# The last eight sums of a graph attention kernel folded into two PSUM banks, and its last softmax stage issued earlier

## The chip, the cores and the metric

One core of a Trainium2 chip runs the program. Times are device microseconds (us); a median is that of three runs. One further execution of each kernel is recorded by the hardware profiler, and the rows of a profile come from that one.

## The reference

What is computed is one pre-norm graph attention layer over 12500 nodes of 128 numbers and 200000 edges, sorted by target, with 64 numbers each. There are 4 heads of 32.

```python
h    = maximum(layernorm(x), 0)                       # 12500 x 128
att  = a1.(W_node h)[src] + a2.(W_node h)[tgt] + a3.(W_edge edge)   # per edge and head
att  = where(att > 0, att, 0.2 * att)
m    = maximum(segment_max(att, tgt), 0)
ex   = exp(att - m[tgt])
den  = segment_sum(ex, tgt) + (200000 - deg) * exp(-m)
out  = x + segment_sum(ex / den[tgt] * (W_node h)[src], tgt)
```

The targets are sorted, so the edges of a node lie side by side, and where a group of edges ends inside a node, the next one continues it. Few edges fall on nodes at the end of the list: there a group of 511 edges touches up to 80 nodes.

## The kernel before, in words

The edges form 392 **groups** of 511 (four chunks of 128 columns each, the first column kept free), and four groups form one of 98 **quads**. Quads are softmaxed together in **supers**: two, two, then four at a time, and at the end 3, 3, 2, 2, 2, 2. The last super, s = 27, is quads 96 and 97; the one before is 94 and 95. All engines' orders are written by hand (`tc.manual_schedule()`): Python generators with `yield` between their steps are interleaved by `together` and `next`, and an engine executes in the order in which its instructions were issued.

The work on an edge has four parts.

*Rows.* A first phase writes the transformed rows of all nodes to a table in DRAM. POOL fetches the rows of an edge chunk by an indirect DMA (L177) into `ga`, which has room for eight quads; some chunks are fetched row by row from the queues of ACT and SP (L785).

*Logits.* For a quad, `all_logits` compares the targets with the nodes of the group's window (DVE L598), multiplies by the targets' shares (PE L604) and by the edge weights (PE L607), adds the pieces (`add_pieces`, DVE L616) and then the shares of the gathered rows (`add_sources`, DVE L628), which gives `U`. `flush` calls `add_sources` for the quad whose logits came last.

*Softmax of a super*, the turned stage (`softmax(s)`, with edges along the free axis): transposes of `U` into `t_ps` (PE L672), times 0.2 (ACT L674), the maximum of the two (DVE L677), a copy of it to `low` (ACT L681), a scan forward and one back with the mask `kp` (DVE L684, L685), which give each node's maximum inside its group; the ends of the groups are turned to one row (PE L695), scanned across the groups (DVE L702, L705) into `into` (L711) and turned back to a column (PE, then DVE copy L725); two more scans (DVE L727, L730) bring in what came from other groups; then the difference (DVE L734), the exponential `ex` (ACT L735), and transposes back (PE L744, L750). `kp` is made by `keeps(s)` from two neighbouring columns of the target list, one of them copied to PSUM first (ACT L653, DVE L655). `run_on(n)` issues n products whose results nobody reads (PE L644): 12 of them behind the ends of the last super, 2 later.

*Sums of a quad* (`sums(q)`): each group's rows are weighed by `ex` (DVE L908), 0/1 marks `hot` say which edge belongs to which node of the window (DVE L936; POOL L882 for the last two quads), and the products of marks and rows are added in a PSUM bank `acc` (PE L948). Row 0 of a bank is what the window's last node has so far; `carry` copies it (ACT L833) into the free first column of the next window's rows and adds the product of that chunk last (PE L840). `summed` copies the finished bank to `pt` (ACT L858) and takes the exponential of -m (ACT L864). `divide` then works out the shares (DVE L1001, L1004, L1006), multiplies (DVE L1010) and adds x (L1014), and the results are written, one window of rows at a time, by `issue` on SP's queue (L545). Windows of the last classes overlap: each is a group's 80 rows from its first node, whatever the number of its nodes, and a later write overwrites what an earlier one left beyond its nodes. The first 22 quads have one window of 80 rows each, those up to quad 35 one of 112 rows, those up to quad 74 one of 112 rows for two groups, and the rest, the last quads among them, a window of 80 rows for each group.

For the end of the program the order is special. In the last super, steps of `softmax` and of `sums(95)` alternate by hand; while `state["held"]` is set, the completion of quad 95's second group waits until the exponential of L735 is issued. The rows of x for quads 95, 96 and 97 are loaded in `sums(95)`. `weigh_last` weighs two groups of quad 97 on POOL (L908 with `last_ex`). A quad's last two groups are divided by themselves, or one by one in quad 97.

## Time and profile before

| | before |
|---|---|
| time, median of 3 runs (lowest to highest) | 1981.34 us (1979.71 to 1984.94) |
| the profiled execution: its time, its span | 1981.96 us, 1980.2 us |
| busy: POOL, PE, DVE, ACT | 1471.8 us (74%), 1338.1 us (68%), 1252.5 us (63%), 337.4 us (17%) |
| mean granted TensorE clock | 0.547 of full speed |
| HBM traffic over the span | 144 GB/s |
| gathers on POOL (L177) | 1463 of 945 ns, 1382.7 us |

The span runs from the first to the last instruction of the profiled execution; its time is 1.8 us more. POOL is the busiest engine and nearly all of its time is the issue of gathers. Over the steady part of the program no engine is above eight tenths in the 40 slices of the page, so what holds is read from the order of waits. The clock of PE is full in parts of the first phase and near the end, and half for most of what lies between.

### The profile page before, as it was taken

How to read it: one execution, taken by the hardware profiler on the slowest of the kernel's cores; microseconds unless marked ns; L12 is line 12 of the kernel's file. 1: busy time of each engine (PE TensorE's matmuls, PEld its weight loads, DVE VectorE, ACT ScalarE, POOL GpSimd, SP SyncE). 2: the span in 40 equal slices, each digit the busy share in tenths (PEclk: the TensorE clock that was granted, in tenths of full speed). 3: DMA queues.
4: the chain of work that ended last, by engine and by line, in shares of the span. 5: the costliest groups of instructions: out<-in, count | busy, mean ns of one | idle time of the engine just before them, and what ended most of it. 6: DMA issues, size and time to landing. Idle time of an engine off the chain costs nothing.

```text
span 1980.2 us, 33747 instructions
## 1 busy us (share of the span) xinstructions
PE 1338.1 (68%) x7385; PEld 1231.8 (62%) x7385; DVE 1252.5 (63%) x3393; ACT 337.4 (17%) x1121; POOL 1471.8 (74%) x1579
## 2 busy tenths in 40 slices
PE   6577786777657666667677576666665666777666
PEld 5466686766646556556566565666565665666655
DVE  6666766765655656557657566566566565667876
ACT  6655010110010100011101101111111011212222
POOL 7767767777777777777777777777777777777774
PEclk8757555555555555555555555555555555555557
DMA  7745655555545545455555555554645555555531
GB/s 257 205 112 123 163 143 136 136 140 165 152 131 165 148 145 151 133 170 152 145 162 147 157 146 158 148 167 135 171 124 134 143 133 137 127 152 128 151 96 34
DMA packets 158958, 288.26 MB, mean 146 GB/s; under 512 B 62488, under 2 KB 106103, under 8 KB 148368
## 3 DMA queue, kind: packets, MB, share of 16 engines
q1 hardware_dynamic: 103326, 174.78, 29.3%
q0 software_dynamic: 49120, 107.44, 23.4%
q10 hardware_dynamic: 6306, 3.85, 0.8%
q8 instruction: 61, 1.00, 0.2%
q14 instruction: 145, 1.19, 0.2%
HBM read 268.71 MB, written 17.19 MB: 144 GB/s over the span
## 4 chain that ended last, share of the span: by engine, by line
PE 29%; DVE 19%; POOL 15%; DMA 13%; issue 13%; ACT 4%; ACTq 4%; DVEq 0%; POOLq 0%
PE acc L948 15%; POOL ga L177 15%; DMA ga<-table,srci 13%; PE lg L607 7%; ACTq L785 3%; DVE at L598 3%; PE acc L840 2%; DVE ga L908 2%; DVE hot L936 2%; DVE t_ps L685 2%; DVE t_ps L684 2%; PE lg L604 1%; DVE t_ps L727 1%; DVE t_ps L730 1%; PE t_ps L672 1%
## 5 line engine op out<-in xcount | busy, mean ns | idle before, releaser
L177 POOL DMA_INDIRECT ga<-table,srci x1463 | 1382.7, 945 | 458.6 <-issue 358.2
L948 PE MATMUL acc<-ga,hot 128*113 128x137 f32 (+1 forms) x2724 | 713.2, 436 | 238.6 <-ACT ga L903 143.8
L948 PEld LDWEIGHTS acc<-ga,hot 128*113 128x113 f32 (+1 forms) x2724 | 589.3, 276 | 263.1 <-ACT ga L903 164.7
L607 PE MATMUL lg<-wblk,ea 128*128 128x8 f32 x1568 | 399.5, 352 | 0.0
L607 PEld LDWEIGHTS lg<-wblk,ea 128*128 128x128 f32 x1568 | 372.0, 301 | 0.0
L604 PEld LDWEIGHTS <-at 112*128 112x128 bf16 (+1 forms) x1568 | 218.4, 164 | 224.7 <-DVE at L598 202.7
L604 PE MATMUL lg<-pw,at 112*128 112x12 bf16 (+1 forms) x1568 | 170.3, 181 | 171.7 <-DVE at L598 171.4
L908 DVE TENSOR_TENSOR ga<-ga,ex_ps 128x528 f32<-128x528 f32 x390 | 269.1, 690 | 21.7 <-PE ex_ps L744 20.7
L598 DVE TENSOR_TENSOR at<-const_ps,db 112x512 bf16<-112x512 f32 (+1 forms) x392 | 264.8, 676 | 0.0
L936 DVE TENSOR_TENSOR hot<-const_ps,slot 128x448 f32<-128x448 f32 (+1 forms) x384 | 212.0, 552 | 0.0
L628 DVE TENSOR_TENSOR U<-const_ps,ga 128x64 f32<-128x64 f32 x98 | 26.1, 266 | 236.2 <-DMA ga<-table,srci 185.7
L840 PE MATMUL acc<-ga,hot 128*81 128x137 f32 (+1 forms) x412 | 133.7, 425 | 18.0 <-ACT ga L833 17.2
L975 DVE SCALAR_TENSOR_TENSOR den_of<-acc,den_of 113x4 f32<-113x4 f32 (+1 forms) x114 | 18.1, 159 | 193.4 <-ACT den_of L855 192.0
L840 PEld LDWEIGHTS acc<-ga,hot 128*81 128x81 f32 (+1 forms) x412 | 98.7, 271 | 26.2 <-ACT ga L833 24.8
L855 ACT ACTIVATE den_of<-acc 113x4 f32<-113x4 f32 (+1 forms) x114 | 19.6, 172 | 537.7 <-PE acc L948 315.6
L744 PE MATMUL ex_ps<-ident,ex 64*128 64x64 f32 (+2 forms) x112 | 18.6, 315 | 114.2 <-ACT ex L735 114.2
L744 PEld LDWEIGHTS ex_ps<-ident,ex 64*128 64x128 f32 (+2 forms) x112 | 13.8, 208 | 116.7 <-ACT ex L735 116.6
L177 POOL DMA_INDIRECT ga<-in_x_dram,srci x72 | 68.5, 952 | 23.2 <-issue 17.1
L833 ACT COPY ga<-acc 1x133 f32<-1x133 f32 x178 | 45.4, 255 | 202.1 <-issue 75.4
L858 ACT COPY pt<-acc 81x137 f32<-81x137 f32 x92 | 24.8, 269 | 219.0 <-PE acc L840 184.2
L435 PE MATMUL row_ps<-wcat,hT 128*128 128x137 f32 x198 | 41.1, 360 | 17.9 <-DVE tgt L441 7.9
L616 DVE TENSOR_REDUCE const_ps<-lg 128x64 f32<-128x192 f32 x98 | 35.0, 358 | 26.4 <-PE lg L607 25.8
(161 smaller groups left out, 1184.1 us busy)
## 6 DMA issues: line engine op xcount, KB each, us to landing
db<-in_dst_dram SPq DMA_DIRECT2D x53, 1024.0 KB
ea<-in_edge_t_dram SPq DMA_DIRECT2D x98, 512.0 KB
by_row<-table ACTq DMA_DIRECT2D x2304, 0.5 KB
db<-in_dst_dram SPq DMA_DIRECT2D x45, 640.0 KB
by_row<-table SPq DMA_DIRECT2D x1664, 0.5 KB
ga<-table,srci POOLq DMA_INDIRECT x1463
table<-row SPq DMA_DIRECT2D x9, 616.5 KB
xt<-in_x_dram SPq DMA_DIRECT2D x9, 576.0 KB
```

What stands on the lines that cost most here:

```text
L177: nc.gpsimd.indirect_dma_start(out=ga[:, i, j, 0:width], out_offset=None, in_=rows, in_offset=bass.IndirectOffsetOnAxis(ap=srci[:, g0 + i, ...
L435: nc.tensor.matmul(row_ps[:, t, :ROW], hT[:, t, :], wcat, start=True, stop=True)
L598: nc.vector.tensor_tensor(at[:span, i, :], node_ps[:span, w0 + i // k:w0 + i // k + 1].to_broadcast([span, GE]), db[:span, i, :], op=OP.is ...
L604: nc.tensor.matmul(lg[:, i, j].rearrange("p k h -> p (k h)"), at[:span, i, j * P:(j + 1) * P], sw, start=i + j == 0, stop=False, skip_grou ...
L607: nc.tensor.matmul(lg[:, i, 2 * w:2 * w + 2, 0, :], ea[:, i, w, :], wblk, start=False, stop=True, skip_group_check=True)
L684: nc.vector.tensor_tensor_scan(raw, same, att, initial=0.0, op0=OP.mult, op1=OP.max)
L785: row = engine.dma_start(as_bytes(to[p:p + 1, :]), rows_at(table, at[p % a_quad], 4 * ROW, 1))
L833: nc.scalar.copy(into, before[0:1, 0:R_CNT + 1])
L840: nc.tensor.matmul(acc, hot[:, i, 0, 0:acc.shape[0]], ga[:, i, 0, :], start=False, stop=stop)
L908: engine.tensor_tensor(val, val, weight.unsqueeze(3).to_broadcast([P, J, H, HW]), op=OP.mult)
L936: nc.vector.tensor_tensor(hot[:, i, :, 1:1 + span], lane_ps[:, 0:span].unsqueeze(1).to_broadcast([P, J, span]), slot[:, g, :].unsqueeze(2) ...
L948: nc.tensor.matmul(acc, hot[:, i, j, 0:1 + span], ga[:, i, j, :], start=new and j == 1, stop=i % k > 1 and i % k == k - 1 and j == J - 1)
```

## The change

Quads 96 and 97 leave `sums` and get a function of their own, `folded`. As before, each of their eight groups has its marks, its weighed rows and its own bank of sums over 81 rows. The bank is now copied to `pt` and multiplied by three 0/1 matrices, `SHIFT`, of 81 x 113: matrix b moves a group's row to the row that its node has in block b of the quad's window, which is 3 blocks of 112 nodes from the quad's first node. The products of a quad's four groups are added in one bank (113 rows, 3 x 137 columns), so that a node that two groups share is complete without a carry between them, and row 0 of the bank is the carry to the next quad. A quad has one exponential, one division and one write of 336 rows (three blocks of 112) in place of those per group. The matrices are made on DVE by comparing a row of lane numbers with the relative place of each node (`relative`, in the earlier check steps), during the sums of quads 92 and 93, in two slots of `ga` that no gather needs any more. x and the output are padded to 12928 rows for these windows.

Beside this: POOL makes the marks for groups 1 to 3 of quad 95 as well, and weighs three groups of quad 97 instead of two, from a copy of the exponentials in SBUF (`XE`). The steps of the last super's turned stage are issued ahead of the steps of `sums(95)` that stood between them: `add_sources` follows `add_pieces` at once, and the rest of `sums(95)`, groups 2 and 3, comes behind the stage. The hold of quad 95's second group is gone. Two steps that stood early are moved or dropped: the copy to `low` of the last super comes behind the two scans, and `keeps` reads the target list without the copy to PSUM for the first and last super. The loads of x for quads 96 and 97 are one each.

```diff
 CLASSES = (22, 4, NARROW), (36, 4, WIDE), (75, 2, WIDE), (None, 1, NARROW)
+FOLDS, PARTS, FREE = 2, 3, 3
...
+        nodes_at = lambda d, at: rows_at(d, at, 4 * D, PARTS * WIDE).rearrange(
+            "(b p) c -> p b c", p=WIDE)
...
+            if q >= first_fold:
+                at = ROWS[q] = windows(base_row, 4 * D, w, 1)
+                due["inputs"].append((as_bytes(xw[1:1 + WIDE, 0:PARTS, :]), nodes_at(x, at[0])))
+                return
...
-            before_ps = ps.tile([SBG * H, GE], F32, name="t_ps")
-            nc.scalar.copy(before_ps[:R], dr[:R, 0:NE + 1])
+            earlier = dr[:R, 0:NE + 1]
+            if 0 < s < len(supers) - 1:
+                before_ps = ps.tile([P, GE], F32, name="t_ps")
+                nc.scalar.copy(before_ps[:R], earlier)
+                earlier = before_ps[:R]
             kp = KP[s] = turned.tile([SBG * H, GE + 1], F32, name="kp")
-            nc.vector.tensor_tensor(kp[:R, 1:GE + 1], dr[:R, 1:NE + 2], before_ps[:R],
+            nc.vector.tensor_tensor(kp[:R, 1:GE + 1], dr[:R, 1:NE + 2], earlier,
                                     op=OP.is_equal)
...
-            raw = run_e if s == len(supers) - 1 else att
+            final = s == len(supers) - 1
+            if not final:
+                nc.scalar.copy(low[:R], att)
+            yield
+            raw = run_e if final else att
             nc.vector.tensor_tensor_scan(raw, same, att, initial=0.0, op0=OP.mult, op1=OP.max)
             nc.vector.tensor_tensor_scan(raw[:, ::-1], same_next[:, ::-1], raw[:, ::-1],
                                          initial=0.0, op0=OP.mult, op1=OP.max)
+            if final:
+                nc.scalar.copy(low[:R], att)
...
-            if state.pop("held", None):
-                complete_window(*begun.pop())
-                divide(*divisions.pop(0))
...
-            if s == len(supers) - 1:
+            if final:
                 run_on(2)
+                XE[s] = turned.tile([P, J, SBG * H], F32, name="xe")
+                nc.scalar.copy(XE[s][:, :, 0:R],
+                               ex_ps[:, 0:J * SBG * H].rearrange("p (j r) -> p j r", j=J)[:, :, 0:R])
...
-            if "held" in state and begun[-1][:2] == (nq - 3, 1):
-                divide(*divisions.pop(0))
-            division = divisions.pop(0) if divisions and "held" not in state else None
+            division = divisions.pop(0) if divisions else None
...
-            parts = {nq - 1: (2, 3), nq - 2: (2,), nq - 3: (2,), nq - 4: (2,)}.get(q, ())
+            parts = (2,) if first_fold - 2 <= q < first_fold else ()
...
-            if q >= nq - FREE:
-                for i in range(m):
+            if q >= first_fold - 1:
+                for i in range(0 if q >= first_fold else 1, m):
...
-            for a in range(nq - 3, nq) if q == nq - 3 else range(q + 1 if q else 0, min(q + 2, nq - 3)):
+            for a in range(q + 1 if q else 0, min(q + 2, first_fold)):
                 fetch_inputs(a)
-            if q == nq - 4:
+            if q == first_fold - 1:
+                for a in range(first_fold, nq):
+                    fetch_inputs(a)
+            if q == first_fold - 2:
                 issue("inputs", all_of=True)
...
-                if q == nq - 1 - FREE and i == 1:
-                    for a in range(nq - FREE, nq):
+                if q == first_fold - 1 and i == 1:
+                    for a in range(first_fold, nq):
                         HOT[a] = marks(a)
-                weigh(i + ahead)
-                if q < nq - FREE:
+                if first_fold - 4 <= q < first_fold - 4 + FOLDS:
+                    shifts(q + 4, i)
+                weighed(nc.vector, ga, i, heads(ex)[:, :, :, g - s0])
+                if q < first_fold - 1 or not i:
                     nc.vector.tensor_tensor(
                         hot[:, i, :, 1:1 + span],
                         lane_ps[:, 0:span].unsqueeze(1).to_broadcast([P, J, span]),
                         slot[:, g, :].unsqueeze(2).to_broadcast([P, J, span]), op=OP.is_equal)
-                if q == nq - 3 and i == 1:
-                    yield
...
-                if (q, i) == (nq - 2, 0):
-                    weigh_last()
-                issue("inputs", "results", *(["inputs"] * 3 if q == nq - 3 else []))
+                issue("inputs", "results", *(["inputs"] * 3 if q == first_fold - 1 else []))
...
+        SHIFT = {}
+        for a in range(first_fold, nq):
+            SHIFT[a] = ga_all[:, (a + 2) % QUADS].rearrange("p g j r -> p (g j r)")[
+                :, 0:QG * PARTS * (1 + WIDE)].rearrange("p (g b c) -> p g b c", b=PARTS, c=1 + WIDE)
...
+        def shifts(q, i):
+
+            to = SHIFT[q][:1 + NARROW, i]
+            R = 1 + NARROW
+            nc.vector.memset(to[:, :, 0:1], 0.0)
+            nc.vector.tensor_copy(to[:, 0, 0:1], ident[:R, 0:1])
+            nc.vector.tensor_tensor(
+                to[:, :, 1:1 + WIDE], lane_ps[:R].unsqueeze(1).to_broadcast([R, PARTS, WIDE]),
+                rel[:R, q - first_fold, i].unsqueeze(2).to_broadcast([R, PARTS, WIDE]),
+                op=OP.is_equal)
+
+        def folded(last_sums):
+            order = [(q, i) for q in range(first_fold, nq) for i in range(quads[q][1])]
...
+            together(last_sums)
+            complete()
+            for q, i in order:
+                on_gpsimd = q == nq - 1 and i < FREE
+                weighed(nc.gpsimd if on_gpsimd else nc.vector, rows[q], i,
+                        heads(XE[s] if on_gpsimd else ex)[:, :, :, quads[q][0] + i - s0])
+                if (q, i) == order[min(1, len(order) - 1)]:
+                    carried_in(first_fold, 0, rows[first_fold], fac if g_fold == s0 else None)
+            while divisions:
+                divide(*divisions.pop(0))
+            banks, accs, pts = {}, {}, {}
+
+            def chunks(q, i):
+
+                bank = ps.tile([P, 512], F32, name="acc", bufs=3)
+                accs[q, i] = bank[0:1 + NARROW, 0:ROW]
+                for j in range(0 if i else 1, J):
+                    nc.tensor.matmul(accs[q, i], HOT[q][:, i, j, 0:1 + NARROW], rows[q][:, i, j, :],
+                                     start=j == (0 if i else 1), stop=i > 0 and j == J - 1)
+
+            def copied(q, i):
+
+                if q not in pts:
+                    pts[q] = work.tile([P, QG, ROW], F32, name="pt", bufs=3)
+                nc.scalar.copy(pts[q][:1 + NARROW, i], accs.pop((q, i)))
+
+            def fold(q, i, last):
+
+                new = q not in banks
+                if new:
+                    banks[q] = (ps.tile([P, 512], F32, name="t_ps") if q == nq - 1 else
+                                ps.tile([P, 512], F32, name="ex_ps", bufs=2))
+                for b in range(PARTS):
+                    nc.tensor.matmul(banks[q][0:1 + WIDE, b * ROW:(b + 1) * ROW],
+                                     SHIFT[q][:1 + NARROW, i, b], pts[q][:1 + NARROW, i],
+                                     start=new and b == 0, stop=last, skip_group_check=True)
+
+            def shares(q):
+
+                acc = banks[q][0:1 + WIDE, 0:PARTS * ROW].rearrange("p (b r) -> p b r", r=ROW)
+                state["before"] = banks[q]
+                den = work.tile([P, QG, H], F32, name="den")[:1 + WIDE, 0:PARTS]
+                nc.scalar.activation(den, acc[:, :, R_SRC:R_SRC + H], AF.Exp, scale=-1.0)
+                return q, acc, den
+
+            def finish(q, acc, den):
+
+                R = 1 + WIDE
+                val = acc[:, :, 0:H * HW].rearrange("p b (h w) -> p b h w", w=HW)
+                nc.vector.scalar_tensor_tensor(
+                    den, acc[:, :, R_CNT:R_CNT + 1].to_broadcast([R, PARTS, H]), float(E), den,
+                    op0=OP.subtract, op1=OP.mult)
+                nc.vector.scalar_tensor_tensor(den, den, -1.0, val[:, :, :, HD],
+                                               op0=OP.mult, op1=OP.add)
+                nc.vector.reciprocal(den, den)
+                res = work.tile([P, QG, D], F32, name="res")[:R, 0:PARTS]
+                nc.vector.tensor_tensor(
+                    res.rearrange("p b (h d) -> p b h d", d=HD), val[:, :, :, 0:HD],
+                    den.unsqueeze(3).to_broadcast([R, PARTS, H, HD]), op=OP.mult)
+                nc.vector.tensor_tensor(res, res, XW[q][:R, 0:PARTS], op=OP.add)
+                due["results"].append((nodes_at(out, ROWS[q][0]), as_bytes(res[1:R])))
+                issue("results", all_of=True)
+
+            waits = []
+            for q in range(first_fold, nq):
+                g0, m = quads[q]
+                for i in range(m):
+                    chunks(q, i)
+                    if i == min(1, m - 1):
+                        if q > first_fold:
+                            carried_in(q, 0, rows[q], fac if g0 == s0 else None)
+                        nc.tensor.matmul(accs[q, 0], HOT[q][:, 0, 0, 0:1 + NARROW], rows[q][:, 0, 0, :],
+                                         start=False, stop=True)
+                        copied(q, 0)
+                    if i:
+                        copied(q, i)
+                    for a in waits:
+                        fold(*a)
+                    if waits and waits[-1][2]:
+                        ended = shares(waits[-1][0])
+                        finish(*ended)
+                    waits = [(q, 0, m == 1)] if i == 0 and m == 1 else [] if i == 0 else [
+                        (q, 0, False), (q, 1, m == 2)] if i == 1 else [(q, i, i == m - 1)]
+            for a in waits:
+                fold(*a)
+            finish(*shares(nq - 1))
...
-            add = nc.gpsimd if nq - 3 <= q <= nq - 2 and lo else nc.vector
-            add.tensor_tensor(res[:, :n, :], res[:, :n, :], xw, op=OP.add)
+            nc.vector.tensor_tensor(res[:, :n, :], res[:, :n, :], xw, op=OP.add)
...
 
                     next(turned_stage)
+                    next(turned_stage)
                     redo = nc.values_load(flag[0:1, 0:1], min_val=0, max_val=1)
                     next(beside[0])
-                    state["held"] = True
+                    next(turned_stage)
+                    next(turned_stage)
                     next(beside[0])
                     next(turned_stage)
                     next(beside[0])
+                    next(turned_stage)
+                    next(turned_stage)
+                    last_sums = beside[0]
+                    beside, turned_stage = [], iter(())
...
-            flush()
-            last_sums = sums(nq - 1)
-            together(last_sums)
-            complete()
-            complete()
+            folded(last_sums)
```

118 lines of the change are left out of this document (70 added, 48 removed).

## The prediction

> **What bounds the kernel now.** I read the page first (busy shares, costliest groups), then the timelines of POOL, SP, DVE, PE and ACT over the last 100 us, the chain that ended last, and the stretches of PE with their clock. In timelines and chain the columns are start, duration (both us), engine, line and tiles; brackets hold the idle time before and what ended it.
>
> ```profile
> span 1980.2 us, 33747 instructions
> ```
>
> ```profile
> 1933.70 0.94 POOL L177 DMA_INDIRECT ga<-table,srci  x1 [0.30 <-issue]
> 1934.69 16.10 POOL L882 TENSOR_SCALAR hot<-lane,slot 128x80 f32<-128x80 f32 x32
> ```
>
> POOL issues the gathers one after another, 0.94 us each with 0.30 us between, and the last ends at 1934.6. The change leaves their number and order alone, so up to there the time is given: what can move is the last 45.6 us. I read them backwards, from SP and DVE:
>
> ```profile
> 1966.82 10.46 SPq L545 DMA_DIRECT2D out_dram<-res  x6
> ```
>
> ```profile
> L545 SPq DMA_DIRECT2D out_dram<-res x16: 316/317/1526, 1936.9 to 1977.0; - x16
> ```
>
> ```profile
> SPq L545 <- DMA out_dram<-res: 22.8, 17, 2.9
> ```
>
> ```profile
> 1970.13 0.29 DVE L1014 TENSOR_TENSOR res<-res,inputs 81x128 f32<-81x128 f32 x1
> ```
>
> The last result is computed at 1970.4, yet the last write is issued at 1977.0. Writes of overlapping rows wait for one another (17 waits, 22.8 us), and the last six are issued (1977.0 - 1966.8) / 5 = 2.04 us apart. So DVE ends 9.8 us before the span does, and 3.2 us of that are the last write and the program's end. Ahead lie the turned stage (the softmax of quads 96 and 97) and their sums:
>
> ```profile
> 1937.46 0.37 DVE L616 TENSOR_REDUCE const_ps<-lg 128x64 f32<-128x192 f32 x1 [1.22 <-PE lg L607]
> ...
> 1940.14 0.26 DVE L628 TENSOR_TENSOR U<-const_ps,ga 128x64 f32<-128x64 f32 x1
> ...
> 1946.68 1.21 DVE L684 TENSOR_TENSOR_SCAN run<-kp,t_ps 32x511 f32<-32x511 f32 x1 [1.40 <-ACT low L681]
> ...
> 1949.77 0.22 DVE L702 TENSOR_TENSOR_SCAN ends<-thru,tops,ex_ps 1x8 f32<-1x8 f32 x1 [0.32 <-PE ex_ps L695]
> ...
> 1950.72 0.25 DVE L711 COPY into<-ends 1x32 f32<-1x32 f32 x2
> ```
>
> ```profile
> 1941.19 1.06 PE L672 MATMUL t_ps<-ident,U 128*32 128x128 f32 x4
> ...
> 1951.23 4.95 PE L644 MATMUL lg<-ones,ident 128*128 128x128 f32 x24
> ...
> 1958.15 1.61 PE L948 MATMUL acc<-ga,hot 128*81 128x137 f32 x12 [0.20 <-issue]
> ```
>
> ```profile
> 1942.29 0.58 ACT L674 ACTIVATE low<-t_ps 32x511 f32<-32x511 f32 x1
> ...
> 1954.85 0.63 ACT L735 ACTIVATE ex<-ex 32x511 f32<-32x511 f32 x1 [3.39 <-DVE ex L734]
> ```
>
> The stage runs from L616 at 1937.5 to the exponential of L735 at 1954.85; the first products of quad 96 start at 1958.15.
>
> **The change, part by part.**
>
> *Writes.* Eight writes of 80 rows become two of 336. Quad 95's four remain; at 2.04 us apart they are through before quad 96's is due, and that one before the last. Only the last stands behind DVE's end.
>
> ```profile
> 1942.48 3.97 SPq L545 DMA_DIRECT2D inputs<-in_x_dram  x8
> ```
>
> ```profile
> 1976.00:1977.00 1.00, 0.00 (x0) 0.00 (x0) 0.00 (x0) 0.00 (x0) 0.00 (x0) 0.50 0.16 41
> ```
>
> The second row is a stretch of one us (busy time of the engines, then clock, DMA share, GB/s): a write of 40 KB keeps the 16 DMA engines busy for 0.16 us. 4.2 times that is 0.67, so the larger write costs 0.5 us more. Bounds: nothing, or 2.0 us, half of what eight loads of 40 KB took in the first row. I take 0.5, since those loads were held by their issue. From DVE's end to the span's: 9.8 becomes 3.2 + 0.5 = 3.7. The loads of x for the two quads become two instead of eight, issued by SP about 20 us before they are read.
>
> *Fold products.* 24 products of 113x137, contracted over 81 partitions, come onto PE; the 32 products that make the sums of the eight groups stay.
>
> ```profile
> 1957.52 0.62 DVE ga L908
> ...
> 1963.88 0.28 ACT pt L858
> ...
> 1964.38 0.16 ACT ga L833
> ...
> 1964.59 0.46 PE acc L840 x2
> 1965.05 0.70 PE acc L948 x6
> ...
> 1966.36 0.22 ACT den L864
> ...
> 1966.61 0.17 DVE den L1001
> ...
> 1966.80 0.18 DVE den L1004
> ...
> 1967.00 0.22 DVE const_ps L1006
> ```
>
> ```profile
> 1967.75 0.42 DVE L1014 TENSOR_TENSOR res<-res,inputs 81x256 f32<-81x256 f32 x1
> ```
>
> Six records are three products: 0.233 us each at the full clock. The moving side of a fold is also 137 wide, so I give it the same price (bounds: half of that, or the 0.46 us of a product that comes alone). 56 x 0.233 = 13.05 us. PE is then full and ACT's copies (0.28 us) hide behind it, with one exception. In the built order the copy of row 0 from quad 96's bank into quad 97 stands behind DVE's multiplication by the shares: 0.22 + 0.17 + 0.18 + 0.22 + 0.55, the copy 0.2, with hand-overs 1.8 us, against 0.93 us of the four products that PE has meanwhile. PE waits 0.85 us. After the last fold come 0.15 us to land, the exponential 0.22, and on DVE 0.17 + 0.18 + 0.22 + two operations on 384 elements at 0.55 each (0.29 for 128, 0.42 for 256), with gaps 1.8. From the first product of quad 96 to DVE's end: 13.05 + 0.85 + 0.15 + 0.22 + 1.8 = 16.1 us, before 1970.4 - 1958.15 = 12.3. A loss of 3.8.
>
> *The turned stage first.* U now follows L616 directly: over at 1937.7 instead of 1940.4, if the gather of quad 97 has landed. Then transposes (0.9), ACT's scaling (0.6), the maximum (0.6), two scans (1.21 each) and the two columns (0.2) end at 1942.6, where L702's row has them ready at 1949.4: ACT's copy between maximum and scan is moved behind the scan, so the wait of 1.40 us goes too. But a weighing (0.62) and a division of quad 94 (0.17 + 0.18 + 0.22 + 0.42 + 0.42, with gaps 1.5) now stand before the 1.2 us from L702 to L711: `into` is ready at 1946.0 instead of 1951.0, 5 us earlier.
>
> Most of that is given back. On ACT the exponential of L735 now queues behind the copy and the exponential of group 1 of quad 95, whose last product queues on PE behind the twelve warming products (L644, 4.95 us) and three products of group 2. PE: 1946.4 + 5.0 + 1.1 = 1952.5; ACT: 0.28, 0.22, hand-overs: 1953.05. DVE has its operand ready at 1950.5, so the queue costs 2.5 us, and the exponential is only 1.8 us earlier than before. From there to the first product of quad 96 it took 3.3 us; now group 3 of quad 95 and two carry rounds (copy 0.16, product 0.46, copy 0.28) lie between, PE waiting for ACT in both: 4.05 us, 1957.1. Net gain 1.05.
>
> *Fold matrices, marks and the copy ahead of kp.*
>
> ```profile
> 1900.27 0.37 DVE L616 TENSOR_REDUCE const_ps<-lg 128x64 f32<-128x192 f32 x1 [2.83 <-PE lg L607]
> 1902.52 0.27 DVE L628 TENSOR_TENSOR U<-const_ps,ga 128x64 f32<-128x64 f32 x1 [1.88 <-DMA ga<-table,srci]
> ...
> 1925.65 0.68 DVE L655 TENSOR_TENSOR kp<-dr,t_ps 32x512 f32<-32x512 int32 x1 [2.15 <-ACT t_ps L653]
> ...
> 1938.72 0.48 DVE L936 TENSOR_TENSOR hot<-const_ps,slot 128x320 f32<-128x320 f32 x1
> ```
>
> ```profile
> 1959.87 2.15 POOL L908 TENSOR_TENSOR ga<-ga,last_ex 128x528 f32<-128x528 f32 x2
> ```
>
> The fold matrices cost DVE eight times one comparison of 81x336 (as L936, 0.48) and two tiny operations: 0.62 us each, 5 us in all, in the sums of quads 92 and 93. Five lie before the waits of 2.83 and 1.88 us that end at 1902.5. Three, 1.9 us, delay the stage of quads 94 and 95; the 2.15 us wait at `kp`, gone with the copy, pays for them. Net 0.4 us earlier at the next L616, counted above; without that cover 1.9 later. POOL makes 44 marks instead of 32 (16.10 / 32 = 0.50 each), until 1956.8, and weighs three groups of quad 97 (1.08 each) until 1960.0; PE asks for the first at 1963, so this hides. The small operations for the relative places lie far before the end, with POOL's gathers as cover.
>
> *Sum.* 1957.1 + 16.1 + 3.7 = 1976.9 against 1980.2: -3.3 us. The profiled execution's own time was 1981.96, 0.6 above the median of 1981.34; on the median the sum gives **1978.0 us**.
>
> **The rivals.** The clock first (the first figures are the stretch and PE's busy time, the third from the end is the clock):
>
> ```profile
> 1941.81:1945.23 3.42, 3.42 (x17) 3.40 (x15) 3.12 (x9) 1.50 (x7) 3.42 (x8) 0.50 0.14 39
> 1945.23:1948.64 3.41, 1.57 (x11) 1.09 (x10) 1.98 (x3) 1.37 (x5) 3.41 (x8) 1.00 0.24 65
> 1948.64:1952.05 3.41, 1.48 (x12) 1.29 (x13) 2.87 (x20) 0.20 (x1) 2.15 (x4) 0.50 0.22 60
> ...
> 1965.71:1969.12 3.41, 1.94 (x13) 1.22 (x11) 2.56 (x11) 1.73 (x8) 0.56 (x1) 1.00 0.09 25
> 1969.12:1972.53 3.41, 0.00 (x0) 0.00 (x0) 1.16 (x6) 0.00 (x0) 0.00 (x0) 1.00 0.09 20
> ```
>
> A stretch with PE busy throughout is followed by the full clock, one with 1.57 us by half, one with 1.94 us by full still. After the change the stretch behind the warming products holds about 1.9 us of PE work, since PE now waits for ACT there.
>
> (1) *The clock falls once* and is back after one full stretch: 1 us on the last group of quad 95 and 1.7 to 3.3 us on the products; by the median about 1982. The Trainium skill, page "TensorE: Matmul & The Clock Gate", section "Part 1: The HAM clock gate (the "warmup" mystery)", takes the clock down after an idle window of about 3.4 us; by that rule it would stay up and the sum as it is. The trace differs: half came after a stretch with 1.57 us of work.
>
> (2) *Slower: the clock stays at half through the folds*, because PE, waiting for copies between them, never fills a stretch. 56 products at 0.46 instead of 0.233 cost 13 us: 1991. It decides for slower by over 0.3% once 9.3 us of products have doubled. Against it: each fold is issued a group behind its sums, so PE should be full.
>
> (3) *Faster*: the allowances all come out at their low ends. The late fold matrices hide in DVE's other waits (-1.5), the clock rises earlier in the warming products (-1.0), the larger write costs nothing more (-0.5), the row copy holds nobody (-0.8): 1974.2.
>
> (4) *The gather holds U*, the wait that would take the place of the copies: quad 95's last gather released U only at 1902.52, 4 us after its issue. The same for quad 97 gives 1938.7, +1 us: 1979.0.
>
> That the writes do not merge I leave out: the built program issues one transfer for each of the two quads.
>
> **How the numbers follow.** Forecast 1978.0: 0.45; (4) 0.07; (1) 0.10; (3) 0.30; (2) 0.08. A measurement here tells some 0.3% (5.9 us) from no change: under 1975.4 is faster, over 1987.3 slower. So faster 0.30 (rival 3), slower 0.08 (rival 2), same 0.62. The range goes from a little under (3), 1973.5, to (1) with the write's upper bound, 1984.0; it leaves out (2) and what lies beyond (3).
>
> **What would show it.** Writes: two behind quad 95's, and the span ending 3.7 us after DVE's last operation. Folds: 24 products of 0.23 us and PE full from 1957 to 1971. Stage: the first scan at 1940 with no wait for ACT, yet the exponential not before 1953, behind an ACT copy that waits for PE. Wrong would be: half clock after 1955; PE gaps between folds; U waiting for a gather; products waiting for POOL's marks.

## The result

The changed kernel takes 1978.78 us, median of 16 runs (1973.59 to 1981.66); the kernel before takes 1985.32 us over 16 runs (1979.71 to 1991.0) beside it. The ratio is 0.9966, with a 95% interval of 0.9954 to 0.9978: 6.5 us less, 4.4 to 9.1 by the interval. The forecast was 1978.0 us (1973.5 to 1984.0) from a gain of 3.3 us; it was taken from the 1981.34 us of three runs. The gain is twice as large, and the kernel before is 4.0 us slower over sixteen runs than over those three: the two cancel, so that the times lie 0.8 us apart is luck. The profiled execution of the changed kernel took 1975.77 us, its span is 1973.9 us, 6.3 less than before. The twelve experiments fell on four chips on which both kernels take 2.77 to 2.85 ms, because engines stand still there for 5 to 20 us at a time (last section), so their ratios are within a chip and their intervals wide.

POOL and SP at the end of the changed kernel (timelines; start, duration, engine, line, tiles):

```profile
1929.49 0.95 POOL L182 DMA_INDIRECT ga<-table,srci  x1 [0.30 <-issue]
1930.47 22.04 POOL L905 TENSOR_SCALAR hot<-lane,slot 128x80 f32<-128x80 f32 x44
```

```profile
1940.30 29.57 SPq L550 DMA_DIRECT2D out_dram<-res  x8
```

The last gather ends at 1930.4, where it ended at 1934.6 before: 4.2 of the 6.3 us are won ahead of the part that the forecast called the only one that can move. The rest of the program, called the tail below, takes 43.5 us in place of 45.6. Its rows on DVE, ACT and PE, those that answer to the ones quoted of before:

```profile
1932.31 0.37 DVE L628 TENSOR_REDUCE const_ps<-lg 128x64 f32<-128x192 f32 x1 [1.22 <-PE lg L619]
1932.72 0.27 DVE L640 TENSOR_TENSOR U<-const_ps,ga 128x64 f32<-128x64 f32 x1
...
1935.45 1.21 DVE L701 TENSOR_TENSOR_SCAN run<-kp,t_ps 32x511 f32<-32x511 f32 x1
...
1945.27 0.67 DVE L753 TENSOR_TENSOR ex<-low,t_ps 32x511 f32<-32x511 f32 x1
...
1968.95 0.56 DVE L1075 TENSOR_TENSOR res<-res,inputs 113x384 f32<-113x384 f32 x1
```

```profile
1948.68 0.27 ACT L882 COPY pt<-acc 81x137 f32<-81x137 f32 x1 [6.44 <-PE acc L849]
1948.98 0.21 ACT L888 ACTIVATE den<-pt 81x8 f32<-81x8 f32 x1
1949.10 0.61 ACT L754 ACTIVATE ex<-ex 32x511 f32<-32x511 f32 x1
...
1961.98 0.26 ACT L859 COPY ga<-ex_ps 1x133 f32<-1x133 f32 x1 [1.34 <-DVE res L1072]
```

```profile
1952.98 1.81 PE L1033 MATMUL acc<-ga,hot 128*81 128x137 f32 x14
...
1955.80 1.57 PE L1049 MATMUL ex_ps<-pt,ga 81*113 81x137 f32 x12
1957.20 1.10 PE L1033 MATMUL acc<-ga,hot 128*81 128x137 f32 x8
...
1962.29 0.46 PE L1087 MATMUL acc<-ga,hot 128*81 128x137 f32 x2 [0.93 <-ACT ga L859]
...
1965.87 1.57 PE L1049 MATMUL t_ps<-pt,ga 81*113 81x137 f32 x12
```

The order is as foreseen. U follows the reduction at once, no wait stands before the scan, and the exponential's operand is ready at 1945.9; the exponential itself starts at 1949.1, behind the copy of quad 95's group 1. The folds cost 0.234 us each (1957.20 - 1955.80 = 1.40 for six). Behind DVE's last operation stands one write.

**Where the other 4.2 us came from.** The first super, before and after (POOL, DVE and ACT of before, then DVE and POOL of after):

```profile
95.53 0.94 POOL L177 DMA_INDIRECT ga<-table,srci  x1 [2.22 <-DMA table<-row]
...
135.90 0.94 POOL L177 DMA_INDIRECT ga<-table,srci  x1 [5.42 <-DVE ga L183]
...
255.70 0.94 POOL L177 DMA_INDIRECT ga<-table,srci  x1 [5.23 <-PE acc L840]
```

```profile
125.89 0.68 DVE L598 TENSOR_TENSOR at<-const_ps,db 80x512 bf16<-80x512 f32 x1
133.18 0.68 DVE L655 TENSOR_TENSOR kp<-dr,t_ps 32x512 f32<-32x512 int32 x1 [6.61 <-ACT t_ps L653]
```

```profile
128.72 3.95 ACT L265 ACTIVATE ga<-ga,shift,rstd 128x128 f32<-128x128 f32 x10
132.58 0.57 ACT L653 CAST t_ps<-dr 32x512 f32<-32x512 int32 x1
```

```profile
125.29 0.67 DVE L670 TENSOR_TENSOR kp<-dr 32x512 f32<-32x512 int32 x1
```

```profile
94.08 0.95 POOL L182 DMA_INDIRECT ga<-table,srci  x1 [0.76 <-issue]
...
247.79 0.94 POOL L182 DMA_INDIRECT ga<-table,srci  x1 [3.39 <-PE acc L849]
```

Before, ACT makes the copy for the first super's mask only after sixteen normalizations (the last ten, 3.95 us, are the first row of its fence). DVE waits 6.61 us for it, and POOL waits behind DVE, since a small memset of DVE's, issued behind the mask, releases its next gather. After, DVE makes the mask from the target list at once. The last gather that waits over 2 us in the whole program waits for a slot of gathered rows that the first sums free: at 255.70 before, at 247.79 after. Behind it the gathers follow one another to the end. So the 6.3 us divide thus: first gather from the table -1.45; from there to the freed slot 160.17 and 153.71, -6.46; from there to the end of the last gather 1678.94 and 1682.65, +3.71; the rest 45.56 and 43.46, -2.10.

Of the +3.71, 3.53 are the gathers' own time: 1343 of them take 1272.71 us in place of 1269.18. On the page a gather takes 948 ns in place of 945, and nothing shows that this is the change's:

```profile
L182 POOL DMA_INDIRECT ga<-table,srci x1463 | 1386.7, 948 | 450.4 <-issue 353.6
```

```profile
L182 POOL DMA_INDIRECT ga<-table,srci x1463 | 1385.1, 947 | 1192.3 <-PE acc L849 568.5
```

```profile
L182 POOL DMA_INDIRECT ga<-table,srci x1463 | 1381.7, 944 | 1190.9 <-PE acc L850 553.2
```

These are the groups of the page of the changed kernel, then of two experiments (after_warm4 and after_best) that ran on one chip: 947 and 944 ns in kernels that have the same gathers. The changed kernel itself has 946 in after_same.

### The profile page after: what moved, and what is told of

Same layout as the page of the kernel before. It is cut to its first block, busy times and chain, and to the rows that moved or that the text cites. A ratio compares the mean times of both kernels' runs of the same rounds, so it can differ in the third digit from the quotient of the medians.

```text
span 1973.9 us, 33834 instructions
## 1 busy us (share of the span) xinstructions
PE 1349.8 (68%) x7433; PEld 1243.3 (63%) x7433; DVE 1254.4 (64%) x3410; ACT 335.0 (17%) x1110; POOL 1481.6 (75%) x1590
## 5 line engine op out<-in xcount | busy, mean ns | idle before, releaser
L616 PEld LDWEIGHTS <-at 112*128 112x128 bf16 (+1 forms) x1568 | 219.9, 165 | 218.3 <-DVE at L610 187.8
L616 PE MATMUL lg<-pw,at 112*128 112x12 bf16 (+1 forms) x1568 | 170.4, 181 | 165.0 <-DVE at L610 156.9
L912 DVE TENSOR_TENSOR ga<-ga,ex_ps 128x528 f32<-128x528 f32 x389 | 268.2, 690 | 21.2 <-PE ex_ps L760 20.7
L879 ACT ACTIVATE den_of<-acc 113x4 f32<-113x4 f32 (+1 forms) x114 | 19.7, 173 | 537.1 <-PE acc L955 318.2
L628 DVE TENSOR_REDUCE const_ps<-lg 128x64 f32<-128x192 f32 x98 | 35.0, 357 | 25.2 <-PE lg L619 24.5
```

The costliest lines, as they stand in the source:

```text
L616: nc.tensor.matmul(lg[:, i, j].rearrange("p k h -> p (k h)"), at[:span, i, j * P:(j + 1) * P], sw, start=i + j == 0, stop=False, skip_grou ...
L628: nc.vector.tensor_reduce(st[:, :m], LG[q][:, :m].rearrange("p g j k h -> p g j h k"), AX.X, OP.add)
L912: engine.tensor_tensor(val, val, weight.unsqueeze(3).to_broadcast([P, J, H, HW]), op=OP.mult)
```

## The experiments

Theory H (the head, the part up to the freed slot): the copy that `keeps` waited for in the first super delayed all up to the freed slot, and the stream of gathers behind it carries the gain to the end; the tail adds the rest. Theory T (tail alone, the forecast's): nothing ahead of the last gather moves, and what the trace shows there is the difference of two executions. "The first weighing" below is the first row of L908 (L912 after, a few lines on in edited kernels), counted from the first gather of the table; in the profiles quoted above it comes at 63.69 us before and at 57.25 after.

| kernel | median us | ratio to before, same chip | first weighing | L628 to first product of quad 96 | to DVE's end | to the span's end |
|---|---|---|---|---|---|---|
| before (first profile) | 1985.32 | | 63.69 | 20.69 | 12.27 | 9.78 |
| after (first profile) | 1978.78 | 0.9966 [0.9954, 0.9978] | 57.25 | 20.67 | 16.53 | 4.39 |
| before_keeps0 | 2822.82 | 0.9982 [0.9961, 1.0003] | 88.18 | | | 9.78 |
| keeps0_again | 2816.04 | 0.9978 [0.9958, 0.9998] | 88.57 | | | 10.00 |
| before_copy_early | 2791.14 | 0.9964 [0.9929, 0.9998] | 88.55 | | | 9.72 |
| before_two_writes | 2823.15 | 0.9979 [0.9951, 1.0008] | 96.93 | | | 4.59 |
| after_same | 2784.59 | 0.9967 [0.9938, 0.9995] | 85.80 | 19.20 | 16.52 | 4.32 |
| after_copy0 | 2822.17 | 0.9971 [0.9945, 0.9997] | 94.45 | 20.16 | 16.53 | 4.41 |
| copy0_again | 2818.31 | 0.9978 [0.9954, 1.0003] | 94.97 | 20.49 | 16.54 | 4.58 |
| after_low0 | 2816.21 | 0.9952 [0.9928, 0.9975] | 88.19 | 20.12 | 16.53 | 4.40 |
| after_best | 2805.95 | 0.9940 [0.9916, 0.9964] | 88.53 | 18.58 | 15.36 | 4.56 |
| after_warm4 | 2810.47 (one run) | | 89.13 | 17.56 | 16.53 | 4.34 |
| after_best2 | 2786.72 | 0.9969 [0.9943, 0.9995] | 85.07 | 19.64 | 15.40 | 4.32 |
| after_fewer_folds | 2779.63 | 0.9939 [0.9905, 0.9973] | 85.84 | 19.47 | 14.11 | 4.42 |

(L628 is the reduction's line in the changed kernel, L616 before. Columns with a profile's times are in us and from one execution each. The experiments ran on four chips, and medians are compared within a chip only: before_keeps0, after_copy0, after_low0 and before_two_writes on one where the kernel before takes 2829.74 us; keeps0_again, copy0_again, after_best and after_warm4 on one with 2823.07; after_same, before_copy_early and after_best2 on one with 2796.95; after_fewer_folds on one with 2795.46.)

### The mask's wait alone: before_keeps0 and keeps0_again

```diff
-            before_ps = ps.tile([SBG * H, GE], F32, name="t_ps")
-            nc.scalar.copy(before_ps[:R], dr[:R, 0:NE + 1])
+            earlier = dr[:R, 0:NE + 1]
+            if s:
+                before_ps = ps.tile([SBG * H, GE], F32, name="t_ps")
+                nc.scalar.copy(before_ps[:R], earlier)
+                earlier = before_ps[:R]
```

> Theory H (the head): in the kernel before, DVE's mask for the first super waits 6.61 us for ACT's copy of the target list, everything that DVE computes up to the first waiting gather of the second round comes later by that, and from there on POOL sets the time. Without that copy alone the kernel before should be 5.1 to 6.6 us faster, ratio 0.9967 to 0.9974. Theory T (the forecast's: up to the last gather nothing moves, and what the trace shows there is the difference of two executions): no change, ratio 0.9990 to 1.0010.

> The kernel before without the copy ahead of the first super's mask, as in before_keeps0, for a chip on which POOL's gathers set the pace as in the first profile. Theory H: 5.1 to 6.6 us faster, ratio 0.9967 to 0.9974, no wait of 5 us on POOL near 130 us, and the bank of rows that POOL waits for near 250 us free 6.6 us earlier. Theory T: ratio 0.9990 to 1.0010.

### The wait taken out, the copy kept: before_copy_early

```diff
                 logits(q, i)
+                if q == 0 and i == 1:
+                    copied_rows(0)
...
-            before_ps = ps.tile([SBG * H, GE], F32, name="t_ps")
-            nc.scalar.copy(before_ps[:R], dr[:R, 0:NE + 1])
+            if s:
+                copied_rows(s)
+            dr, before_ps = DR.pop(s), BEFORE.pop(s)
```

> The kernel before with the same copy to PSUM ahead of the first super's mask, issued about a quad's logits earlier on ACT, ahead of the sixteen normalizations that it queued behind. The copy stays, its wait should go. Theory H (it is the wait): 5 to 6.6 us faster, as without the copy, and the first weighing of the first super about 88.6 us behind the first gather from the table in place of 95.5. Rival (the copy itself, or a mask read from PSUM, is what costs): no change.

The mask's rows of before_two_writes (whose head is that of before), of before_keeps0 and of before_copy_early:

```profile
189.49 0.68 DVE L655 TENSOR_TENSOR kp<-dr,t_ps 32x512 f32<-32x512 int32 x1 [6.61 <-ACT t_ps L653]
```

```profile
181.42 0.67 DVE L658 TENSOR_TENSOR kp<-dr 32x512 f32<-32x512 int32 x1
```

```profile
183.66 0.67 DVE L663 TENSOR_TENSOR kp<-dr,t_ps 32x512 f32<-32x512 int32 x1
```

On these chips too the wait is 6.61 us with the late copy and none without it, and none with the copy made early. The first weighing comes at 94.45 to 96.93 in the three kernels that wait and at 85.07 to 89.13 in those that don't. On the first of the four chips it is 96.93 and 94.45 against 88.18 and 88.19, on the second 94.97 against 88.57, 88.53 and 89.13. The slot that the first sums free follows it (POOL of before_two_writes, then of before_keeps0):

```profile
278.38 0.94 POOL L177 DMA_INDIRECT ga<-table,srci  x1 [16.84 <-PE acc L840]
```

```profile
269.50 0.94 POOL L177 DMA_INDIRECT ga<-table,srci  x1 [16.05 <-PE acc L843]
```

Behind the first gather of the table that is 142.02 and 132.49 us, 9.5 less without the wait, and 137.47 and 130.67 in copy0_again and after_warm4 of the second chip. So the wait is what delays the head. That it is the wait, and neither the copy nor a mask read from PSUM, rests on before_copy_early alone, which has both and comes at 88.55; no kernel with the wait was profiled on its chip, where the changed kernel comes at 85.80.

By time the three ratios, weighted by their intervals, give 0.9977 (0.9964 to 0.9991), some 6.3 us (2.5 to 10.2) of 2.82 ms: a ratio of 1 is outside, theory H's 5.1 to 6.6 us inside, and the interval's end touches the lower edge of what theory T allows (0.9990). The size at the end of a run on a chip like the first profile's was not measured by itself; there the trace's -6.46 stands for it.

### The change without its gain in the head: after_copy0 and copy0_again

```diff
-            if 0 < s < len(supers) - 1:
+            if s < len(supers) - 1:
```

> The changed kernel with the copy ahead of the first super's mask put back, all else as changed. Theory H: only the gain of the tail is left, 2.1 us by the traces (3.3 by the forecast): ratio 0.9983 to 0.9990, and POOL idle for 5 us before one gather near 130 us again. Theory T: as the changed kernel, ratio about 0.9966.

> The changed kernel with that copy put back, as in after_copy0. Theory H: only the tail's 1.2 to 2.1 us are left, ratio 0.9989 to 0.9994. Theory T: as the changed kernel, ratio 0.9966. The two parts together should give the whole: keeps0_again and this one add up to 0.9966 within their intervals.

The wait of 6.61 us is back in both, and so are the late first weighing and POOL's wait on DVE's memset: some 55 us behind the first gather POOL waits 5.49 us for it in both, 5.48 in before_two_writes, and not at all at that place in the kernels without the copy's wait. In the traces the mechanism is as theory H has it. The times are weaker: 0.9971 lies nearer to theory T's 0.9966 than to theory H's 0.9983, 0.9978 lies halfway between 0.9966 and 0.9989, and each interval holds both. keeps0_again and copy0_again together make 0.9956, which is 0.9966 within their intervals. The ratios together give 0.9975 (0.9957 to 0.9993), 2 to 12 us, where the tail alone would be 0.9993 to 0.9996 of 2.82 ms. So the times of this pair decide nothing between the theories. If the gain is larger than the tail's, what it can hold beside is the first gather from the table, which comes 0.6 to 2.9 us sooner in kernels of the changed kind than in those of the kind before on the same two chips (134.15 and 135.36 against 136.36 and 137.01 us; 133.09, 135.35 and 135.41 against 136.02), as 94.08 against 95.53 in the first profiles. On a third chip it is 131.93 and 133.05 against 139.32 in before_copy_early. Why is open: no edit was tried on it.

### The changed kernel on such a chip: after_same

No edit.

> The changed kernel as it is, beside the others on one chip. Theory H: the head's 6.6 us and the tail's 1.2 to 2.1 us add up, 7.8 to 8.7 us less than the kernel before, ratio 0.9969 to 0.9972 where the kernel before takes 2.82 ms and 0.9956 to 0.9966 where it takes 1.98 ms. Theory T: the tail alone, 0.9990 to 0.9996.

0.9967 is in the middle of what theory H says for both kinds of chip. The interval reaches to 0.9995 and so does not exclude T by itself. Against T speaks the first weighing, 85.80 us, where the kernels with the wait have 94.45 at the least, though on two other chips.

### The writes: before_two_writes

```diff
             due["results"] += [(rows_at(out, ROWS[q][lo + i], 4 * D, span),
-                                as_bytes(res[1:R, i, :])) for i in range(n)]
+                                as_bytes(res[1:R, i, :])) for i in range(n)
+                               if q < nq - 2 or lo + i == QG - 1]
```

> The kernel before with six of the eight writes of quads 96 and 97 left out (the rows of groups 0 to 2 of both are not written; all is computed). The forecast's term for the writes says that they stand 2 us apart and cost 9.8 - 3.7 = 6.1 us at the end: ratio 0.9967 to 0.9971, and DVE's last operation 3.2 us before the end. The rival, that most of the 9.8 us is the landing of the last write, says 1 us at most: ratio over 0.9990.

The last operation of DVE and the last writes of SP, in its timelines:

```profile
2808.62 0.29 DVE L1014 TENSOR_TENSOR res<-res,inputs 81x128 f32<-81x128 f32 x1
```

```profile
2794.70 14.55 SPq L545 DMA_DIRECT2D out_dram<-res  x6
```

The last write is issued from 2808.94 on, right behind DVE's end at 2808.91, and the span ends 4.59 us after DVE in place of 9.78: the queue of writes cost 5.2 us, not the landing of the last. The ratio, 0.9979 (0.9951 to 1.0008), decides nothing here; the trace does. The 0.5 us that the forecast gave the larger write did not show: with a write of 40 KB last there are 4.59 us, with one of 168 KB 4.32 to 4.58. What was mis-sized is the end from the start of the last issue on: 3.2 us as the forecast read it behind a queue of writes (1976.96 to 1980.2), but 4.56 here (2808.94 to 2813.5) and 4.36 in the changed kernel (1969.54 to 1973.9), where it stands alone. Why a write of the same 40 KB stands further from the end when it is alone is open.

### The folds: after_fewer_folds

```diff
-                for b in range(PARTS):
+                for b in range(PARTS if new else 1):
```

> The changed kernel with the fold products of a quad's groups 1 to 3 cut to the first block (12 of 24 left out, so blocks 1 and 2 hold group 0 alone and the last rows of both quads are not the reference's). The forecast prices a fold at 0.233 us with PE full: from the first product of quad 96 to DVE's end 16.5 us falls by 12 x 0.233 = 2.8 to 13.7 us. Rival (ACT's copies or DVE's divisions hold the folds, the products hide): under 1 us of it.

From the first product to DVE's end it takes 14.11 us in place of 16.53, 2.4 for the 2.8 expected: the folds are on the path, at about the price that the forecast gave them.

```profile
2757.18 0.46 PE L1087 MATMUL acc<-ga,hot 128*81 128x137 f32 x2 [0.94 <-ACT ga L859]
...
2760.30 1.01 PE L1049 MATMUL t_ps<-pt,ga 81*113 81x137 f32 x4
```

The wait for row 0 stays (0.94), and the last two folds take 1.01 us, where two products of 0.234 at PE's pace would be through after 0.5: with so few folds the last one seems to wait for ACT's copy (2760.50 to 2760.77), which would be the rest of the 0.4.

### Fewer unread products: after_warm4

```diff
             if s == len(supers) - 1:
-                run_on(12)
+                run_on(4)
```

> The changed kernel with 4 unread products in place of 12 behind the last ends. Queue theory: PE is free 8 x 0.46 = 3.7 us earlier, the exponential 2.8 us earlier, and the span from L628 of quad 97 to the end falls from 41.6 to about 39. Clock theory (rival 1 and 2 of the forecast): without a full stretch the clock stays at half at first, the products of quads 96 and 97 take 0.46 us for part of the way, and that span grows to 43 to 52 us.

The queue theory's number came: 38.43 us from L628 to the end, the exponential 13.68 us behind L628 (16.79 in the changed kernel). PE's clock still rose in time:

```profile
2779.59 2.08 PE L656 MATMUL lg<-ones,ident 128*128 128x128 f32 x8
2781.46 1.58 PE L955 MATMUL acc<-ga,hot 128*81 128x137 f32 x6
...
2785.77 0.87 PE L955 MATMUL acc<-ga,hot 128*81 128x137 f32 x6
```

Three products take 1.58 us before the rise and 0.87 after. The 3.4 us before the rise held 3.00 us of PE work here, four unread products and group 2. It is one execution, and the rise is not at a fixed place: in the changed kernel the full clock came 15.6 us behind L628 in the first profile and 12.8 us in after_same, and in after_low0, after_copy0 and copy0_again, with the same tail, at 14.7, 14.8 and 15.5. The first of the tail's columns goes with it, from 19.20 to 20.67.

### Three waits more taken out: after_low0 and after_best

```diff
             final = s == len(supers) - 1
-            if not final:
+            behind = final or not s
+            if not behind:
                 nc.scalar.copy(low[:R], att)
             yield
-            raw = run_e if final else att
+            raw = run_e if behind else att
...
-            if final:
+            if behind:
                 nc.scalar.copy(low[:R], att)
```

> The changed kernel, and in the first super also the copy to low behind the two scans, as in the last. DVE waits 2.79 us for that copy at 137.6 us in the trace of the changed kernel, and POOL 3.39 us for a bank of gathered rows at 243.5 us. Theory H: the first wait goes, POOL's wait falls to about 0.6 us, and the kernel is 2.8 us faster than the changed one: ratio 0.9950 to 0.9955. Theory T: as the changed kernel.

The scan's wait for the copy is gone, and the ratio fits, but not by the cause given: on this chip DVE then waits 10.63 us at the next scan for nothing that the profile shows (7.71 us at the same place in before_keeps0), the first weighing stays at 88.19, and POOL waits 15.7 us for the slot at 266.54 us. So what this edit is worth where POOL sets the pace stays open.

after_best has this edit and two in the tail:

```diff
                     if i == min(1, m - 1):
-                        if q > first_fold:
-                            carried_in(q, 0, rows[q], fac if g0 == s0 else None)
...
                         ended = shares(waits[-1][0])
+                        carried_in(q, 0, rows[q], fac if g0 == s0 else None)
                         finish(*ended)
...
                     next(turned_stage)
+                    next(turned_stage)
                     next(beside[0])
-                    next(turned_stage)
                     next(turned_stage)
                     last_sums = beside[0]
```

> The changed kernel with three waits more taken out: the first super's copy to low behind its scans (POOL's wait at 243.5 us from 3.39 to about 0.6 us, -2.8); group 2 of quad 95 behind the last exponential, so that this no longer queues behind ACT's copy of group 1 (exponential 3 us earlier, PE's transposes 1.1 us earlier); row 0 of quad 96 copied ahead of its division (PE's wait of 0.93 us gone). Theory H and the queue as read: 4.8 us faster than the changed kernel, ratio to the kernel before 0.9940 to 0.9945. Rival: the exponential is not what the tail waits for, since PE is busy with the warming products until 1947.3 us and group 2 behind them: then only 0.9 of the 2.0 us in the tail come, ratio 0.9945 to 0.9950.

```profile
2780.11 0.63 ACT L755 ACTIVATE ex<-ex 32x511 f32<-32x511 f32 x1 [3.47 <-DVE ex L754]
```

```profile
2781.39 0.90 PE L956 MATMUL acc<-ga,hot 128*81 128x137 f32 x6
2782.13 0.39 PE L850 MATMUL acc<-ga,hot 128*81 128x137 f32 x2
2782.45 0.43 PE L761 MATMUL ex_ps<-ident,ex 32*128 32x32 f32 x4
...
2785.68 1.81 PE L1034 MATMUL acc<-ga,hot 128*81 128x137 f32 x14
...
2793.89 0.40 PE L1086 MATMUL acc<-ga,hot 128*81 128x137 f32 x2
```

The exponential now waits for DVE alone (13.01 us behind L628), and the carry of row 0 no longer waits, which takes 1.17 us from the products' phase (15.36 for 16.53). The transposes come at 15.35 instead of 17.45 and 15.98 in the two profiles of the changed kernel. From L628 to the end it is 38.50 us, against 40.04 to 41.61 in the five profiles with the changed kernel's tail. The full clock is no reason for that: it came 13.9 us behind L628, later than in after_same with its 40.04. The ratio of 0.9940 is the lowest together with that of after_fewer_folds, which leaves work out; as the changed kernel ran on another chip, that after_best is faster than it is shown in the tail's trace and not by a time.

### One step further: after_best2

```diff
                     next(turned_stage)
                     next(turned_stage)
-                    next(beside[0])
                     next(turned_stage)
+                    next(beside[0])
                     last_sums = beside[0]
...
-                run_on(12)
+                run_on(8)
```

(against after_best)

> after_best with 8 unread products in place of 12 and PE's transposes of the exponentials ahead of group 2 of quad 95. In the trace of after_best the exponential is done at 2780.7 us, 16.6 us before the last fold's start, and the transposes wait until 2782.45 behind warming products and group 2. If the transposes are what the rest waits for, the span from L628 of quad 97 to the end falls from 38.5 to about 37, and the kernel is 1.4 us faster than after_best. Rival: DVE's weighings and the carries of quad 95 take over, and nothing or a loss of up to 1 us comes of it, or the clock rises later for want of a full stretch (2 to 5 us more).

```profile
2779.62 0.16 DVE L1137 SCALAR_TENSOR_TENSOR den<-pt,den 81x8 f32<-81x8 f32 x1 [1.76 <-ACT den L889]
2779.82 1.00 DVE L1140 SCALAR_TENSOR_TENSOR den<-den,pt 81x8 f32<-81x8 f32 x1
...
2781.89 1.31 DVE L913 TENSOR_TENSOR ga<-ga,ex_ps 128x528 f32<-128x528 f32 x2
```

The transposes come 1.65 us sooner (13.70 behind L628), and the first product of quad 96 a whole us later (19.64 for 18.58): the rival. The weighing of quad 96 stands on DVE behind the division of quad 95. That now waits 1.76 us for an exponential of ACT and holds one operation of 1.00 us where 0.17 is usual (why is open), so the weighing starts 18.85 us behind L628, and 17.54 in after_best. To the end it is 39.36 us in place of 38.50.

## Why the prediction was right, and where not

The range held and most of the tail went as described, but the gain was too small by what happened elsewhere, and the time came out near by luck: 3.2 us more gain and a kernel before that is 4.0 us slower than the forecast took it for. By the forecast's own bound of 0.3% the result, 0.34% with an interval from 0.22 to 0.46, lies just beyond the edge between "same" (0.62) and "faster" (0.30).

- **What bounds the kernel.** The step that failed is this: "The change leaves their number and order alone, so up to there the time is given: what can move is the last 45.6 us." Number and order were unchanged, but not the moment from which POOL can run without a wait. It is set by the first supers' work, and DVE's 6.61 us for `kp` lay on that path: 6.46 us were won there, of which the slower gathers took 3.71 back. The forecast looked at one wait of this copy, the 2.15 us of the last supers at 1925, and priced it at the tail; it did not look for the other super that the edit touches.
- **Writes.** Right in kind: 9.78 became 4.39, for 3.7 forecast. From the start of the last issue to the end it is 4.36 us and not 3.2, and the 0.5 for the size did not show.
- **Fold products.** 16.53 us for 16.1, with a wait of 0.93 us for row 0 where 0.85 was worked out.
- **The turned stage.** Net gain of 1.05 us forecast: L628 comes 0.95 us sooner behind the last gather (1.87 for 2.82 us), and from it to the first product of quad 96 it takes 20.67 for 20.69, together 0.97. That the total fits is luck: 0.4 was to come ahead of L628 (by its own terms it should be 2.15 - 1.9, nearer 0.3) and 0.65 behind it. Behind it the twelve unread products took 5.49 us where 5.0 was counted (4.95 before, where the clock rose during them). The queue of the exponential was 3.2 us (1945.94 to 1949.10) for 2.5.
- **The sum.** -2.1 us for -3.3 in the tail; the difference is the end behind DVE (0.7), the folds (0.4) and the stage (0.1).
- **The rivals.** The clock did not fall: the stretch behind the warming products held 2.29 us of PE work, and the next one stayed full. The rule of the Trainium skill that the forecast cites (page "TensorE: Matmul & The Clock Gate", section "Part 1: The HAM clock gate (the "warmup" mystery)") leads to the same here, since no window was idle. That the clock held is in part luck all the same, and the three rows of the forecast are no rule. In the trace of before, cut into 577 stretches of 3.41 us on the grid of the forecast's rows, it changes only from one stretch to the next. Of 15 full-clock stretches with PE busy for 0.60 to 0.75 of the time, as the 2.29 of 3.41 here, 9 were followed by half clock and 6 by full; of 162 half-clock stretches with PE busy for 0.98 or more, 24 were followed by full. PE's busy time alone does not tell when the clock changes.

```profile
1944.43:1947.85 3.42, 3.42 (x17) 3.42 (x17) 2.73 (x6) 0.00 (x0) 3.42 (x8) 0.50 0.00 0
1947.85:1951.26 3.41, 2.29 (x22) 2.01 (x21) 1.90 (x6) 1.93 (x7) 3.41 (x9) 0.99 0.00 0
1951.26:1954.67 3.41, 2.90 (x24) 2.49 (x23) 1.94 (x5) 1.45 (x7) 3.41 (x6) 1.00 0.10 26
```

Half clock through the folds did not come, nor a gather that holds U (0.68 us from the reduction's start to U's end). Products did wait for POOL's marks once, 0.35 us at 1938.94, ahead of the unread products. Rival 3's 1974 is nearest to the profiled execution's 1975.77, but by another way: of its four allowances the larger write's came out and the fold matrices' perhaps in part (L628 0.55 us earlier than forecast), while the clock rose no earlier and the row copy held PE for 0.93 us.

## What to carry to other kernels

When an engine streams without a wait to the end, look for its last wait, however early, and for what set that: what is won ahead of it comes out at the end as long as the stream stays without a wait. Here that rests on the first pair of traces; in the experiments POOL waits again and again. When an edit changes a helper that runs at many places, list its calls and look up each wait in the trace. A small operation on a shared queue costs what stands in front of it: 0.57 us of copying cost 6.6 us here, because sixteen normalizations came first.

## What the runs showed of the hardware that was not expected

On the chips of the experiments the program takes 2.77 to 2.85 ms, with the same instructions and nearly the same durations of single operations (a weighing 690 ns, a gather 946 in after_same, 690 and 948 in the first profile). The time goes into stretches of some 5 to 20 us in which engines stand still; the longest group is 735 us of ACT in 69 waits before one instruction (L879). In the rows below, of the changed kernel in after_same, ACT's queue holds at its row-by-row transfers:

```profile
1016.16 1.85 ACTq L804 DMA_DIRECT2D by_row<-table  x6
...
1021.84 10.76 ACTq L804 DMA_DIRECT2D by_row<-table  x5
1032.65 0.30 ACT L823 COPY ga<-by_row 128x137 f32<-128x137 f32 x1 [13.27 <-DMA ga<-table,srci]
```

Six issues take 1.85 us and the next five of that line 10.76. PE, DVE and POOL then wait in turn, and POOL no longer sets the pace. What holds the queue was not tried.

The issue of a gather took 944 to 948 ns on average from one execution to the next. Between the first two profiles, 945 and 948, that makes 3.5 us over 1343 gathers in a row, more than half of what the change is worth.
